# Attention scores of a two-layer graph network: from matmuls on TensorE to a broadcast read from DRAM

## The chip, the cores and the metric

One core of a Trainium2 chip runs the whole kernel as one program. The engines are TensorE (PE, with its weight loads as PEld), VectorE (DVE), ScalarE (ACT), GpSimd (POOL) and SyncE (SP, which issues most transfers). Each engine works through its own queue of instructions in order; semaphores make one wait for another. The metric is device time in microseconds (us) for one execution.

## The reference, cut to what matters

There are 128 independent graphs with 128 nodes and 512 features each, in float32. Layer 0 is an attention over the neighbours of each node with 8 heads of 64 units; layer 1 is two hypergraph convolutions (512 to 1024 to 512) with a layer norm between.

```python
h = relu(layernorm(x))
feats = einsum('bnf,hfu->bhnu', h, W)
e_self = einsum('bhnu,hu->bhn', feats, a_self)
e_neigh = einsum('bhnu,hu->bhn', feats, a_neigh)
dense = leaky_relu(e_self[..., :, None] + e_neigh[..., None, :], 0.2)
dense = dense + NEG_BIG * (1.0 - adj[:, None])
att = softmax(dense, axis=-1)
x = x + relu(einsum('bhij,bhju->bhiu', att, feats) + b)
...
h = relu(layernorm(x))
h = layer_norm(relu(hypergraph_conv(h, adj, W1, b1)), gamma, beta)
x = x + (hypergraph_conv(h, adj, W2, b2) + h_in)
```

Here `h_in` is the h that enters layer 1. The score of head h for the pair of nodes (i, j) is e_self[h, i] + e_neigh[h, j]: an outer sum of two vectors of 128 numbers, made 8 times for each graph.

## The kernel before, in words

**Tiling.** One graph's 128 nodes are the 128 partitions. The attention layer works graph by graph; the hypergraph products work on pairs of graphs (G = 2), with seven block products instead of eight (called u1 to u7 in the first convolution, v1 to v7 in the second). Transposes between a row layout and a column layout go out to DRAM and back in 32x32 blocks: `send` (L484) writes a tile to a DRAM buffer, `fetch` (L493) reads it back with four transfers, `turn` (L506) finishes with DVE's block transpose. This happens to x (the normalized input), p (the softmax), o (the attention output) and r (the hidden layer). For the first DIRECT = 4 graphs and the last LAST ones (p 1, o 1, r 2), `turn` transposes on PE instead.

**Stages of one graph's attention**, by the names that the program gives them: x.load, x.stats, x.rstd, x.relu, x.send, x.fetch, x.turn; f (features, L586: h times W, with 2 x 4 extra columns in each of two halves that give e_self and e_neigh, so 264 columns a half); f.keep (L605: copies the extra columns into a padded tile `pad` and adds the bias into `feats`); e (L626: two transposes of `pad` on PE into eT); e.keep (L635: ACT copies one half into lt, DVE spreads the other into rt); d (L646: four matmuls of 256 columns with only 4 rows each, which add e_self and e_neigh); d.leaky (L666: three ACT passes out of PSUM into sc); d.mask (L674: one POOL add over 1024 columns); d.max (L679: DVE); d.exp and d.exp1 (L684: four Exp passes each); p.send, p.fetch, p.turn; av (L701); av.keep; o.send, o.fetch, o.turn, o.scale, o.add; h.stats, h.rstd, h.relu; z (L743); z.keep; h.add. Each pair adds mask and adjacency stages (mask, adj.*, k) and then the u stages, r.* (hidden layer and its norm), the v stages, and y with its end, `finish` (L946), which also stores the result.

**What sets the order.** The program holds a written-out order. `Order.issue` sorts all stage calls by a number, the place; each engine's queue then holds its instructions in that order. A stage's place for graph n is origin(n) + AT[stage] - sooner. origin(n) is taken from EARLY for the first eight graphs and grows by STEP for each later one; `sooner` is a shift for the first eight graphs (EARLY) and the last six (LATE), by groups of stages. A pair's u, r, v and y stages count from its second graph. The places look like microseconds but nothing waits for a time: they only sort. AFTER (near the end) names which stage has to be called before which.

**Queues.** All transfers, apart from four small rows at the start, are issued by SP, in the order of the places; a send that waits for ACT holds back what stands behind it in SP's queue. TensorE's results lie in PSUM: two banks `ps` that take turns (eT, one part of d, av, z, k, y), a pair of banks `pa` for f and two parts of d, and one bank each for ux, uy, vx, vy (uy or vy also takes a part of d). `feats` has two buffers, `sc` and `pp` one each.

Of the kernel before, what the change touches and what calls it, by code (L numbers as in the profile page):

```python
# [8 lines left out]
F32 = mybir.dt.float32  # L9
# [4 lines left out]
P = 128  # L14
B = 32
# [6 lines left out]
STEP = 19.7  # L22
EARLY = (
    (0, 13.83, 4.99, -3.31, -3.04, -66.56, 23.21, -21.35, -34.93),
    (17.06, 0, 1.56, -0.25, 0, 0, -1.12, -1.26, -1.28),
    (36.59, -0.54, 0, -1.88, -4.09, 11.41, -6.28, -13.24, -68.42),
    (56.49, 0, 16.45, -0.83, 0.38, 0.91, -2.88, -0.08, 3.76),
    (76.1, 0, 0, 0.08, 0.74, -32.13, 32.09, -40.74, -57.65),
    (95.89, -1.62, 5.45, -1.16, 0.13, 0.13, -0.2, 0.28, 0.32),
    (115.32, 0.32, -1.01, 1.31, -0.55, 40.63, 8.4, 17.26, 34.97),  # L30
    (135.24, 2.35, 25.05, 0, 0.25, -0, -0.65, 0, -0.15),
)
LATE = (
    (0, 0, 0, 0, 0, 43.36, 50.78, 44.34),
    (0, 0, 0, -1.28, 0, -2.85, 0, -0.14),
    (0, 0.06, 0.98, 0, 14.76, 8.78, 15.66, 13.25),
    (0, -22.78, 0.48, 0.07, 0.26, -1.59, 0.58, -9.89),
    (0, 0, 1.37, 1.02, 15.36, 13.93, 15.82, 32.72),
    (0, 30.96, 0, -0.45, 0.41, -3.7, -0.45, 0.35),
)  # L40
AT = {
    "x.load": -21.95,
    "x.stats": -15.53,
    "x.rstd": -15.44,
    "x.relu": -11.99,
    "x.send": -10.87,
    "x.fetch": -6.75,
    "x.turn": -5.54,
    "f": 0,
    "f.keep": 3.07,  # L50
    "e": 3.77,
    "e.keep": 3.98,
    "d": 5.46,
    "d.leaky": 6.85,
    "d.mask": 8.25,
    "d.max": 12.88,
    "d.exp": 13.13,
    "d.exp1": 15.17,
    "p.send": 18.81,
    "p.fetch": 20.77,  # L60
    "p.turn": 26.6,
    "av": 29.3,
    "av.keep": 29.4,
    "o.send": 30.82,
    "o.fetch": 36.22,
    "o.turn": 37.55,
    "o.scale": 38.14,
    "o.add": 39.38,
    "h.stats": 42.94,
    "h.rstd": 43.02,  # L70
    "h.relu": 46.17,
    "z": 47.93,
    "z.keep": 51.23,
    "h.add": 51.55,
    "mask.load": -34.65,
    "mask": -21.04,
    "adj.load": -17.12,
    "adj.turn": 13.46,
    "adj.weigh": 17.47,
    "k": 31.81,  # L80
    "k.keep": 38.44,
    "us1": 55.2,
    "us2": 57.58,
    "us3": 55.55,
    "us4": 90.13,
    "u1": 62.85,
    "u1.keep": 70.95,
    "u6": 70.97,
    "u6.keep": 81.26,
    "u2": 76.62,  # L90
    "u2.keep": 78.73,
    "r.aL": 80.04,
    "u5": 83.04,
    "u7": 85.42,
    "u7.keep": 85.87,
    "r.bR": 87.8,
    "u4": 90.51,
    "u4.keep": 95.81,
    "r.bL": 95.88,
    "u3": 90.17,  # L100
    "u3.keep": 92.23,
    "r.aR": 96.21,
    "rb.send": 96.61,
    "rb.stats": 100.31,
    "ra.send": 97.96,
    "ra.stats": 103.65,
    "rb.fetch": 97.63,
    "rb.turn": 102.59,
    "ra.fetch": 101.17,
    "ra.turn": 113.63,  # L110
    "vs1": 112.44,
    "vs3": 117.81,
    "vs2": 120.57,
    "vs4": 137.15,
    "v1": 129.15,
    "v1.keep": 132.3,
    "a1": 133.76,
    "b1": 135.65,
    "b0": 138.73,
    "v6": 140.65,  # L120
    "v6.keep": 141.58,
    "v2": 136.71,
    "v2.keep": 138.23,
    "v5": 144.57,
    "v7": 142.98,
    "v7.keep": 145.72,
    "v4": 152.85,
    "v4.keep": 154.38,
    "v3": 150.71,
    "v3.keep": 151.98,  # L130
    "ya": 161.01,
    "ya.keep": 163.25,
    "yb": 180.67,
    "yb.keep": 182.25,
}
W2_AT = (36.61, -1.28, -6.75, 45.49, 48.27, 57.8, 58.95, 1.45, 76.16, 0.51, 7.04, 6.43, -21.07, -10.31, 0.29, -7.07, -4.88, -5.39)
DIRECT = 4
LAST = {"x": 0, "p": 1, "o": 1, "r": 2}
# [18 lines left out]
def gat_then_hypergraph_kernel(  # L157
# [24 lines left out]
    QH = H // 4  # L182
# [4 lines left out]
    E = 2 * HB  # L187

    const = ctx.enter_context(tc.tile_pool(name="const", bufs=1))
    io = ctx.enter_context(tc.tile_pool(name="io", bufs=11))  # L190
# [56 lines left out]
    for key, v, tile_, at in (  # L247
# [11 lines left out]
    we_sb = wk.tile([P, P], F32, tag="lt", name="we_sb", bufs=1)[:, 0 : KF * 2 * E].rearrange(  # L259
        "p (k b c) -> p k b c", k=KF, b=2  # L260
    )
# [29 lines left out]
    cm = const.tile([P, F], F32, name="cm")  # L291
# [13 lines left out]
    def score_weights(k):  # L305
        for t in range(2):
            prod = wk.tile([P, 2, FB], F32, tag=("xn", "zT")[t], name=f"prod_{t}_{k}", bufs=(1, 3)[t])
            (nc.vector, nc.gpsimd)[t].tensor_tensor(
                prod,
                w0_sb[:, k, :, 0:FB],  # L310
                (a_bc[0], an_bc)[t].rearrange("p (b c) -> p b c", b=2),
                ALU.mult,
            )
            nc.vector.tensor_reduce(
                we_sb[:, k, :, t * HB : (t + 1) * HB],
                prod.rearrange("p b (h u) -> p b h u", u=U),
                AX.X,
                ALU.add,
            )
# [6 lines left out]
    def bias_rows(key, out):  # L326
        spreads.add(key)
        for q in range(out.shape[1] // F):
            t = psum(f"{key}_{q}")
# [3 lines left out]
    def turn_gb():  # L333
        t = psum("gb_ps")
# [4 lines left out]

    EW = P + QH
    pads = []
    for i in range(2):
        pad = const.tile([P, 2 * EW], F32, name=f"pad_{i}")
        nc.vector.memset(pad, 0.0)
        nc.vector.memset(
            pad[:, 0:P].rearrange("p (q y) -> p q y", y=32)[:, :, QH : 2 * QH], 1.0
        )
        nc.vector.memset(  # L350
            pad[:, P : 2 * P].rearrange("p (q y) -> p q y", y=32)[:, :, 0:QH], 1.0
        )
        pads.append(pad)
    dh = const.tile([P, QH], F32, name="dh")
    iq = ident.rearrange("p (q y) -> p q y", y=32)
    for j in range(QH):
        nc.vector.tensor_reduce(
            dh[:, j : j + 1], iq[:, :, j : 2 * QH : QH], AX.XY, ALU.add
        )
    diag = const.tile([P, QH, P], F32, name="diag")  # L360
    nc.vector.tensor_copy(diag, dh.unsqueeze(2).to_broadcast([P, QH, P]))
# [8 lines left out]
    NF = 2  # L370
# [4 lines left out]
    def second_rows():  # L375
        assert "gbT" in sw
        t = psum("sw_ps")[0:2]
# [11 lines left out]
    def second_spread():  # L389
        for i, key in enumerate(("cm", "bw")):  # L390
            sw[key] = psum(f"{key}_ps")
# [7 lines left out]
        nc.scalar.copy(bw_bc, sw["bw"])  # L399
        nc.scalar.mul(cm, sw["cm"], 1.0 / DH)  # L400
# [3 lines left out]
    def second_weights(k):  # L404
        assert "cm" in sw
        sw["centred"] = sw.get("centred", 0) + 1
        nc.vector.scalar_tensor_tensor(
            w2_sb[:, k], w2_sb[:, k], gbT[:, k : k + 1], cm, ALU.mult, ALU.subtract
# [44 lines left out]

    def norm_rstd(n, key):

        mv = sm.tile([P, 2], F32, tag="mv", name=f"mv_{key}{n}")
        nc.vector.bn_aggr(mv, S[n].pop("st" + key))  # L457
# [17 lines left out]
    def direct(n, key):  # L475
        return n < DIRECT or n >= N - LAST[key]

# [6 lines left out]
    def send(n, key, rows, k):  # L484
# [6 lines left out]
        nc.sync.dma_start(d, rows.rearrange("p (b c) -> p b c", b=NB))  # L491
# [14 lines left out]
    def turn(n, key, k, tag, bufs=2):  # L506
        rows = S[n].pop(key + "r")
        S[n][tag] = wk.tile([P, k, P], F32, tag=tag, name=f"{tag}_{n}", bufs=bufs)
        if direct(n, key):
            for q in range(k // 4):  # L510
                t = psum(f"{key}t_{n}_{q}")
# [49 lines left out]
    def adj_keep(g):  # L561
        s = SP[g]
        k_ps = s.pop("k_ps")
        s["kk"] = gp.tile([P, G, P], F32, tag="kk", name=f"kk_{g}", bufs=5)
        nc.scalar.copy(s["kk"], k_ps[:, :, 0:P])

# [38 lines left out]
    def keep_features(n):  # L605
# [3 lines left out]
        pad = pads[n % 2]  # L609
        for t in range(2):  # L610
            nc.vector.tensor_copy(
                pad[:, t * EW : t * EW + P]
                .rearrange("p (b q y) -> p b q y", b=2, y=32)[:, :, :, 0:QH],
# [584 lines left out]
```

## Time and profile before

| what | value |
|---|---|
| median of 3 runs | 2672.8 us (2669.91 to 2674.42) |
| profiled execution, own time | 2671.91 us |
| its span, first to last instruction | 2670.1 us |
| granted TensorE clock, mean | 0.993 |
| busy: PE, PEld, DVE, ACT, POOL | 2611.1, 1799.3, 1907.0, 1500.8, 1855.5 us |
| f (L597), 2048 PE instructions | 486.1 us |
| d (L658), 1024 PE instructions | 92.4 us |
| eT (L631), 256 PE instructions | 49.5 us |
| mask add (L677), 128 POOL instructions | 303.0 us, 2367 ns each |
| DMA moved | 478.5 MB, 179 GB/s mean |

How to read it: the busy time of an engine is the time in which at least one of its instructions ran, so overlapping instructions count once; "mean ns of one" counts each in full. A float32 matmul appears as two instructions: f is written as 8 matmuls and has 16 records a graph. A line of a group names the line of the program, the engine, the operation, the tile written and those read, the shapes, the count, then the busy time, the mean of one, and the idle time of the engine just before such instructions with what ended it. A line of the timeline gives the start, the length and the number of merged instructions. A line of waits gives the total, the number of times and the longest.

### The profile page before, as it was taken

The page shows a single profiled execution, that of the slowest core. Times are in us where ns is not written, and L with a number is a line of the kernel's source. Part 1 is how long each engine was busy: PE and PEld are TensorE (multiplying, and loading weights), DVE is VectorE, ACT ScalarE, POOL GpSimd, SP SyncE. Part 2 cuts the span into 40 slices and gives each one's busy share as a digit, 9 for nine tenths or more (in the row PEclk, how much of TensorE's full clock was granted, in tenths as well). Part 3 has the DMA queues.
Part 4 walks back from the last instruction along what each step waited for, and adds up shares of the span by engine and source line. Part 5 has one row for each costly group of instructions (what it writes and reads, how often), then busy time and mean ns, then how long its engine had stood idle before and what let it go on. Part 6 is the DMA issues. An engine that isn't in the chain of part 4 may idle for free.

```text
span 2670.1 us, 42320 instructions
## 1 busy us (share of the span) xinstructions
PE 2611.1 (98%) x12461; PEld 1799.3 (67%) x12461; DVE 1907.0 (71%) x3554; ACT 1500.8 (56%) x4948; POOL 1855.5 (69%) x2196
## 2 busy tenths in 40 slices
PE   8799999999999999999999999999999999999999
PEld 4466667666667666667666666667666667667666
DVE  4667777777777776777777776777776777777763
ACT  3555556556556555556555555556556556556542
POOL 5676767767767767767767767767767767767763
PEclk8899999999999999999999999999999999999999
DMA  3246656666666666566566566566566566666541
GB/s 111 81 126 194 192 182 199 193 181 194 190 189 196 182 195 195 182 190 199 184 190 198 180 196 194 182 195 195 179 197 196 175 204 196 180 196 194 177 133 59
DMA packets 501616, 478.51 MB, mean 179 GB/s; under 512 B 135797, under 2 KB 404101, under 8 KB 501386
## 3 DMA queue, kind: packets, MB, share of 16 engines
q1 hardware_dynamic: 501376, 475.80, 58.9%
q8 instruction: 99, 1.62, 0.3%
q14 instruction: 131, 1.07, 0.1%
q10 hardware_dynamic: 10, 0.01, 0.0%
HBM read 248.86 MB, written 226.75 MB: 178 GB/s over the span
## 4 chain that ended last, share of the span: by engine, by line
PE 60%; DMA 17%; SPq 8%; DVE 7%; ACT 5%; issue 2%; POOL 1%; DVEq 0%; ACTq 0%; POOLq 0%
PE f L597 12%; PE uy L855 8%; SPq L502 7%; PE vy L855 7%; PE vx L855 6%; DMA pm<-pd 6%; PE uz L855 5%; PE ux L855 5%; PE vz L855 4%; DMA xd<-xn 3%; PE av L707 3%; PE y L946 3%; DMA pd<-pp 2%; DMA rd<-r 2%; PE z L747 2%
## 5 line engine op out<-in xcount | busy, mean ns | idle before, releaser
L597 PE MATMUL f<-w_sb,hT 128*128 128x264 f32 (+1 forms) x2048 | 486.1, 391 | 10.7 <-DVE hT L521 9.6
L597 PEld LDWEIGHTS f<-w_sb,hT 128*128 128x128 f32 x2048 | 391.7, 193 | 113.2 <-issue 34.9
L691 ACT ACTIVATE pp<-sc,nmx 128x128 f32<-128x128 f32 x1024 | 396.8, 391 | 98.6 <-DVE nmx L682 98.6
L677 POOL TENSOR_TENSOR sc<-sc,at 128x1024 f32<-128x1024 f32 x128 | 303.0, 2367 | 62.8 <-ACT sc L672 62.6
L855 PE MATMUL vx<-w_sb,rT 128*128 128x256 f32 x1024 | 248.3, 385 | 0.5 <-DVE rT L519 0.4
L855 PE MATMUL ux<-w_sb,zT 128*128 128x512 f32 x512 | 240.6, 592 | 0.0
L639 ACT COPY lt<-eT 128x128 f32<-128x128 f32 x128 | 34.0, 266 | 355.1 <-PE eT L631 355.1
L733 POOL TENSOR_TENSOR xt<-xt,o 128x512 f32<-128x512 f32 x128 | 163.0, 1274 | 99.0 <-DVE o L729 54.1
L459 POOL TENSOR_SCALAR ve_a<-mv_a 128x1 f32<-128x1 f32 x128 | 28.4, 222 | 272.2 <-DVE mv_a L457 258.0
L855 PEld LDWEIGHTS vx<-w_sb,rT 128*128 128x128 f32 x1024 | 184.7, 190 | 33.3 <-issue 11.8
L521 DVE STREAM_TRANSPOSE pT<-pm 128x1024 f32<-128x1024 f32 x123 | 152.9, 1243 | 66.8 <-DMA pm<-pd 62.4
L691 ACT ACTIVATION_READ_ACCUMULATOR pp<-sc,nmx 128x1 f32 x1024 | 193.9, 189 | 0.0
L790 ACT ACTIVATE sq<-r,nm 128x512 f32<-128x512 f32 x256 | 182.7, 714 | 4.2
L773 ACT ACTIVATE r<-aL 128x512 f32<-128x512 f32 x64 | 40.4, 631 | 253.7 <-DVE aL L866 253.7
L831 POOL TENSOR_TENSOR rT<-rT,rT 128x512 f32<-128x512 f32 x64 | 81.5, 1274 | 137.7 <-DVE rT L521 119.6
L682 DVE TENSOR_REDUCE nmx<-sc 128x8 f32<-128x1024 f32 x128 | 155.3, 1213 | 28.0 <-POOL sc L677 27.7
L765 POOL TENSOR_TENSOR xt<-xt,b_bc 128x512 f32<-128x512 f32 x128 | 163.1, 1274 | 10.0
L521 DVE STREAM_TRANSPOSE hT<-xm 128x512 f32<-128x512 f32 x124 | 88.0, 710 | 114.7 <-DMA xm<-xd 114.6
L469 ACT ACTIVATE h<-xt,nmr_b,rstd_b 128x512 f32<-128x512 f32 x128 | 103.2, 806 | 114.9 <-POOL nmr_b L464 114.9
L764 POOL TENSOR_TENSOR xt<-xt,h 128x512 f32<-128x512 f32 x128 | 163.2, 1275 | 5.2 <-ACT h L469 5.2
L747 PEld LDWEIGHTS z<-kk,h 128*128 128x128 f32 x1024 | 134.6, 193 | 40.4 <-issue 24.8
L641 DVE TENSOR_TENSOR rt<-diag,eT 128x256 f32<-128x256 f32 x128 | 51.9, 405 | 153.6 <-ACT lt L639 153.6
(165 smaller groups left out, 6441.6 us busy)
## 6 DMA issues: line engine op xcount, KB each, us to landing
pd<-pp SPq DMA_DIRECT2D x123, 512.0 KB, 3.8
pm<-pd SPq DMA_DIRECT2D x492, 128.0 KB, 3.7
rd<-r SPq DMA_DIRECT2D x122, 512.0 KB, 3.7
rm<-rd SPq DMA_DIRECT2D x488, 128.0 KB, 3.1
xt<-in_x SPq DMA_DIRECT2D x128, 256.0 KB, 2.9
out<-xt SPq DMA_DIRECT2D x128, 256.0 KB, 2.8
xd<-xn SPq DMA_DIRECT2D x124, 256.0 KB, 2.2
xm<-xd SPq DMA_DIRECT2D x496, 64.0 KB, 2.0
```

The source lines that it names most:

```text
L502: nc.sync.dma_start(m[b * B : (b + 1) * B], d[:, b, :].rearrange("(a x) r -> x a r", x=B))
L521: nc.vector.transpose(S[n][tag].rearrange("p k (a x) -> p k a x", x=B), S[n].pop(key + "m").rearrange("p a (k y) -> p k a y", y=B),)
L597: nc.tensor.matmul(s["f"][:, b, cols], hT[:, k, :], weights[:, k, b, :], start=(k == 0), stop=(k == KF - 1),)
L677: nc.gpsimd.tensor_tensor(s["sc"], s["sc"], neg.to_broadcast([P, H, P]), ALU.add)
L682: nc.vector.tensor_reduce(s["nmx"], s["sc"], AX.X, ALU.max, negate=True)
L691: nc.scalar.activation(blocks(n, "p", s["pp"])[:, h], sc[:, h, :].rearrange("p (b y) -> p b y", y=B), AF.Exp, bias=nmx[:, h : h + 1], accu ...
L733: nc.gpsimd.tensor_tensor(s["xt"], s["xt"], s.pop("o").rearrange("p k c -> p (k c)"), ALU.add)
L747: nc.tensor.matmul(s["z"][:, k * P : (k + 1) * P], s["h1"][:, k * P : (k + 1) * P], SP[n // G]["kk"][:, n % G, :], start=True, stop=True,)
L764: nc.gpsimd.tensor_tensor(s["xt"], s["xt"], s["h1"], ALU.add)
L765: nc.gpsimd.tensor_tensor(s["xt"], s["xt"], b2_bc, ALU.add)
L790: nc.scalar.activation(sq, s["r"][:, q * 512 : (q + 1) * 512], AF.Square, bias=nm[:, 1:2], accum_out=ss[:, q : q + 1],)
L855: nc.tensor.matmul(p[w + bank][:, 0:cols], left[:, k, :], right[:, k, :], start=(first and k == 0), stop=(k == kb - 1), skip_group_check=n ...
```

## The change

The scores are no longer made on PE.

1. The extra columns of f are sorted differently: the first half of f carries e_self of all 8 heads, the second half e_neigh of all 8 (E stays 8). f.keep copies e_self into a small tile `es`. Stage e is now one DVE block transpose of e_neigh's 32 last columns, straight out of PSUM. e.send (SP) writes the 16 KB to DRAM; e.fetch (SP, two transfers) reads 4 heads x 128 numbers, 2 KB, into every one of the 128 partitions, 256 KB each, as the tiles sc (halves, three buffers). The two transposes on PE, `pad`, lt, rt, diag and the four d matmuls are gone.
2. leaky is 8 ACT passes of 128x128 with e_self as the bias, in place in sc. Mask, maximum and Exp work by halves of four heads, so that the second half can follow the first.
3. `send` (x, p, o, r) is issued by ACT. e.send, all fetches, loads and the stores of the result stay with SP; the store of the result is a stage of its own.
4. DIRECT is now 4 for x, p and o and 2 for r, and no last graph is transposed on PE (LAST is gone).
5. Some one-time weight work uses other PSUM banks; `feats` has three buffers in place of two, `io` (the x tiles) 12 in place of 11; norm means, degrees and the hidden norm's root are stages of their own.
6. All places are new: STEP is 19.25 instead of 19.7, EARLY, LATE, AT and W2_AT have new numbers.

```diff
-STEP = 19.7
+STEP = 19.25
...
 AT = {
-    "x.load": -21.95,
+    "x.load": -19.25,
...
-    "x.send": -10.87,
-    "x.fetch": -6.75,
-    "x.turn": -5.54,
+    "x.send": -12.05,
+    "x.fetch": -9.3,
+    "x.turn": -3.58,
     "f": 0,
-    "f.keep": 3.07,
-    "e": 3.77,
-    "e.keep": 3.98,
-    "d": 5.46,
-    "d.leaky": 6.85,
-    "d.mask": 8.25,
-    "d.max": 12.88,
-    "d.exp": 13.13,
-    "d.exp1": 15.17,
-    "p.send": 18.81,
-    "p.fetch": 20.77,
-    "p.turn": 26.6,
-    "av": 29.3,
+    "e": 2.18,
+    "f.keep": 5.65,
+    "e.send": 4.8,
+    "e.fetch": 8.85,
+    "d.leaky": 11.65,
+    "d.leaky1": 12.71,
+    "d.mask": 12.49,
+    "d.mask1": 14.25,
+    "d.max": 14.4,
+    "d.max1": 15.7,
+    "d.exp": 15.25,
+    "d.exp1": 17.1,
+    "p.send": 19.43,
+    "p.fetch": 24.45,
+    "p.turn": 29.56,
+    "av": 33.41,
...
-    "o.send": 30.82,
-    "o.fetch": 36.22,
+    "o.send": 39.2,
+    "o.fetch": 51.02,
...
-    "z": 47.93,
+    "z": 71.55,
...
-    "u1": 62.85,
+    "u1": 81.64,
...
-    "v1": 129.15,
+    "v1": 142.38,
...
-    "yb": 180.67,
-    "yb.keep": 182.25,
+    "yb": 183.16,
+    "yb.keep": 186.01,
+    "yb.store": 186.48,
 }
...
-DIRECT = 4
-LAST = {"x": 0, "p": 1, "o": 1, "r": 2}
+DIRECT = {"x": 4, "p": 4, "o": 4, "r": 2}
...
     def direct(n, key):
-        return n < DIRECT or n >= N - LAST[key]
+        return n < DIRECT[key]
...
     def send(n, key, rows, k):
...
-        nc.sync.dma_start(d, rows.rearrange("p (b c) -> p b c", b=NB))
+        nc.scalar.dma_start(d, rows.rearrange("p (b c) -> p b c", b=NB))
...
     def turn_e(n):
         s = S[n]
-        s["eT"] = psum(f"eT_{n}")
...
+        s["eT"] = sm.tile([P, B], F32, tag="eT", name=f"eT_{n}", bufs=2)
+        nc.vector.transpose(s["eT"], s["f"][:, 1, FB + E - B : FB + E])
+
+    def send_e(n):
+        s = S[n]
+        s["ed"] = dr.tile([B, NB, B], F32, tag="ed", name=f"ed_{n}")
+        nc.sync.dma_start(s["ed"].rearrange("y b x -> b y x"), s.pop("eT"))
+
+    def fetch_e(n):
+        s = S[n]
+        ed = s.pop("ed")
+        s["sc"] = []
+        for part in range(2):
+            sc = wk.tile([P, HB, P], F32, tag="sc", name=f"sc_{n}_{part}", bufs=3)
+            nc.sync.dma_start(
+                sc.rearrange("p h j -> p (h j)"),
+                ed[B - H + part * HB :][0:HB]
+                .rearrange("(o y) b x -> o (y b x)", o=1)
+                .to_broadcast([P, HB * P]),
+            )
+            s["sc"].append(sc)
+
+
+    def leaky(n, part):
+        s = S[n]
+        for j in range(HB):
+            h = part * HB + j
+            sc = s["sc"][part][:, j]
+            nc.scalar.activation(sc, sc, AF.Prelu, bias=s["es"][:, h : h + 1], alpha=SLOPE)
+
+    def mask(n, part):
+        sc = S[n]["sc"][part]
         neg = SP[n // G]["neg"][:, n % G : n % G + 1, :]
-        nc.gpsimd.tensor_tensor(s["sc"], s["sc"], neg.to_broadcast([P, H, P]), ALU.add)
...
+        nc.gpsimd.tensor_tensor(sc, sc, neg.to_broadcast([P, HB, P]), ALU.add)
...
-        nc.sync.dma_start(out[n], s.pop("xt"))
+
+    def store(n):
+        nc.sync.dma_start(out[n], S[n].pop("xt"))
```

## The prediction

> **What bounds the kernel now.** I read the busy times first, then the slices, then TensorE's (PE's) own groups, then its instructions in order of time, and last the queues.
>
> The page's busy times, the slices of PE and its clock, and the shares of the chain that ended last:
>
> ```profile
> PE 2611.1 (98%) x12461; PEld 1799.3 (67%) x12461; DVE 1907.0 (71%) x3554; ACT 1500.8 (56%) x4948; POOL 1855.5 (69%) x2196
> ...
> PE   8799999999999999999999999999999999999999
> ...
> PEclk8899999999999999999999999999999999999999
> ...
> PE 60%; DMA 17%; SPq 8%; DVE 7%; ACT 5%; issue 2%; POOL 1%; DVEq 0%; ACTq 0%; POOLq 0%
> ```
>
> PE is busy for 98% of the span and idle for 59 us in all; only the first slices (the fill) are below nine tenths. A stretch of the steady part says the same (columns: length, then busy time and count of PE, PEld, DVE, ACT, POOL, then clock, DMA share, GB/s):
>
> ```profile
> 1200.00:1600.00 400.00, 397.40 (x1915) 275.28 (x1913) 293.45 (x550) 231.26 (x769) 285.18 (x337) 1.00 0.63 191
> ```
>
> PE lacks 2.6 of 400 us; the next engine, VectorE (DVE), has 107 us free. So the steady part ends when PE's queue ends, and what is taken off PE comes off the time until the next engine or a wait takes over. The ninth product f starts at 161.78 us and the 128th at 2557.39: 2395.6 / 119 = 20.13 us for one graph.
>
> **What the change takes off PE.** The two groups that go, and where they stand in time (start, length):
>
> ```profile
> L658 PE MATMUL d<-rt,lt 4*128 4x256 f32 x1024 | 92.4, 430 | 5.2 <-DVE rt L641 5.2
> L631 PE MATMUL eT<-ident,pad 128*128 128x128 f32 x256 | 49.5, 275 | 8.0 <-DVE pad L611 8.0
> ```
>
> ```profile
> 1317.27 0.38 PE L631 MATMUL eT<-ident,pad 128*128 128x128 f32 x2
> 1317.48 1.88 PE L855 MATMUL uz<-w_t,us 128*128 128x512 f32 x4
> 1319.30 0.71 PE L658 MATMUL d<-rt,lt 4*128 4x256 f32 x8
> 1319.94 1.98 PE L855 MATMUL uy<-w_sb,zT 128*128 128x512 f32 x4
> 1321.76 1.05 PE L747 MATMUL z<-kk,h 128*128 128x128 f32 x8
> ...
> 1325.61 1.88 PE L855 MATMUL uz<-w_sb,us 128*128 128x512 f32 x4
> 1327.32 1.88 PE L855 MATMUL uy<-w_t,zT 128*128 128x512 f32 x4
> 1329.04 0.61 PE L557 MATMUL k<-hmb,hmT 128*128 128x129 f32 x4
> ```
>
> Busy time alone gives (92.4 + 49.5) / 128 = 1.11 us for a graph, but matmuls overlap, so I take distances between starts. eT holds the queue from 1317.27 to 1317.48, 0.21 us; d from 1319.30 to 1319.94, 0.64. An ordinary block of four takes 1.72 (1325.61 to 1327.32 to 1329.04), but the one ahead of d takes 1.82 (1317.48 to 1319.30) and the one behind it 1.82: d costs 0.10 more on each side. Together 0.21 + 0.64 + 0.20 = 1.05 us, between 0.85 (no side costs) and 1.11 (busy). **128 x 1.05 = -134 us** (bounds -109 and -142). Nothing is put on PE in their place; f keeps its 264 columns, since E is 8 before and after. The transposes on PE that DIRECT and LAST ask for become fewer: those of the last p (two blocks of four), o (one) and two r (four), and of r for graphs 2 and 3 (four). Eleven blocks at 0.44 us (8 took 2642.44 to 2643.31) are **-5 us**.
>
> **What it puts elsewhere, for each graph.**
> - ScalarE (ACT): it loses lt (0.27) and the three leaky passes (1.0 from start to end in the queue), and gains eight passes of 128x128 with a bias. The nearest rows are L549 (0.68 for two) and L691 (0.39 each with its accumulator): 2.7 to 3.1. It gains four DMA issues. SP needs 0.34 for such a one, ACT's own in the trace took 0.22 to 0.52: 0.9 to 2.1. ACT goes from 231.3 / 400 x 20.13 = 11.6 us to 14.0 to 15.6.
> - GpSimd (POOL): one mask add of 2.37 becomes two of 512 columns, 1.27 each by the row L764: 14.4 + 0.2 = 14.6.
> - DVE: two pad copies (0.24) and rt (0.41) go; a copy of es (0.16), a transpose of 128x32 (between 0.13 and the 0.43 of the 128x256 one, L536) and one more start of a maximum (0.1) come: 14.8 stays 14.8.
> - DMA: SP's and ACT's transfers use 0.63 x 20.13 = 12.7 us of all 16 engines. The queue's own line
>
> ```profile
> q1 hardware_dynamic: 501376, 475.80, 58.9%
> ```
>
> gives 475.8 MB / (0.589 x 16 x 2670 us) = 18.9 KB per us of one engine, and 50 ns a packet. Two fetches of 256 KB are 524 / (16 x 18.9) = 1.7 us, 128 small packets of e.send 0.4: 14.8.
>
> At 19.1 us for a graph these are 73 to 82% (ACT), 76, 77 and 77%: all under PE's 100, so I price them at nothing beyond the new waits below. The cover is PE's queue; without it, the surplus over 19.1 us would count 128 times.
>
> **The new path to the scores.** Before, f reaches leaky by pad, eT, lt, rt, d. Now: DVE's e at f's end, e.send on SP (0.34 and a landing; the row am, also of 128-byte pieces, lands in 2.6), two e.fetch (0.4 each, landing as xt, 2.9): about 7.5 us from f to the first leaky, against 3.1 before (f ends at 1316.57, leaky starts at 1320.37 behind another pass). Behind e.fetch on SP stands x.fetch, and behind leaky on ACT stand exp, p.send and av.keep: if the row is late, the next f and av are late. The places leave room: e.fetch stands 4.05 behind e.send with p.fetch's four issues between, leaky 2.8 behind e.fetch, and av 33.4 behind f where it was 29.3; feats gets a third buffer for it. Between 0 and the full 4.4 us a graph (a path with no room), I take 0 for the path itself.
>
> By the Trainium skill, "DMA: Bandwidth & Descriptors", section "Why a DMA increments its semaphore by 16 and not by 1", a transfer is split over no more engines than divide both sides' outermost sizes, and e.send writes with the outermost size 4. At 50 ns a packet that would be 1.6 us in place of the 0.4 of 16 engines, my estimate from the row above and that rule; no row here shows it, and it would be 1.2 us of the room.
>
> **Sends in ACT's queue.** SP now waits in its own order for what ACT has yet to finish:
>
> ```profile
> SPq L491 <- ACT oT L718: 212.4, 122, 3.5
> SPq L491 <- ACT xn L469: 165.5, 114, 34.2
> SPq L491 <- ACT r L773: 86.9, 59, 9.4
> ```
>
> On ACT the data were written by the same engine, so these 465 us of SP's waiting go, while ACT pays the issues counted above. SP is 8% of the chain and PE covers it, so I value this at 0. The same page, section "Rules for kernel authors", speaks against the move: issuing from several engines saves only issue time, since all run on the same DMA engines. By it the gain is 0 as well, but the three rows show that waiting in order is what SP sheds.
>
> **Fill and drain.** The first u1 stood at place 79.9 and started at 93.72; its place is now 101.3, 21.3 later. The first v1 goes from 147.5 (started 159.60) to 162.0, 14.5 later. u and v take 7 blocks of 1.72 a pair each, 6.0 a graph, so PE work of 21.3/20 x 6.0 + 14.5/20 x 6.0 = 10.8, with z 12 us, moves from the fill, where PE has gaps, to behind the last f: **+12** (bounds 0, if the fill closes up, and 24). At the end the last r went over PE (0.87 and a copy); now send (3.7), four issues (1.8), landing (3.1) and a transpose (1.2) take 8 us more. The previous pair's v products (12 us) stand in between: **+8** (0 to 16).
>
> **New waits in the steady part.** All places are new and the others' loads rise from 58 to 74% to 73 to 82%. PE idled 14.5 us between 400 and 2400, 0.15 a graph. I add 0.2 for each of 120 graphs: **+24** (bounds 0 and the 1.05 saved, 126).
>
> **Sum**, on the profiled execution's 2671.9 us (0.9 under the median of the runs, 2672.8): 2671.9 - 134 - 5 + 12 + 8 + 24 = **2577 us**, about 3.6% faster.
>
> **Rivals.**
> 1. Another order takes PE's place: DVE, POOL and ACT each stand in one queue, and one late landing holds all behind it. For it: in the first 200 us PE waits for DVE (pad 7.0, rt 5.2 us), so such waits exist. Against: in the steady part only 0.7% is lost at 74%. If half the saving is given back, 0.5 us x 126 more, the time is 2577 + 63 = 2640.
> 2. Slower: the broadcast fetch. 128 partitions read one 2 KB row, which no row here shows. If it costs k times the queue's mean, DMA needs 12.7 + 0.4 + 1.7k; it passes today's 20.13 at k = 4.1 and then sets the pace. At k = 4.5 it is 20.8, and the time 2672 + 0.7 x 120 + 20 (fill and drain) = 2776. For it: DMA is the second largest user and it already reaches eight tenths in some slices of 10 us. Against: p's 512 KB land in 3.8 us.
> 3. No change: the path from f to the scores sets the graph's pace at just 20.1 us, 2673. Little speaks for a hit within 0.2%, which is about what a measurement of this kernel can tell from no change.
>
> **Chances.** Forecast 0.56 (its own range 2540 to 2615), rival 1 0.23, rival 2 0.18, rival 3 0.03. Faster 0.79, same 0.03, slower 0.18. The range for 8 in 10 runs from 2535, where fill, drain and waits cost little, to 2680, past rivals 1 and 3; rival 2 is left out.
>
> **What would show it.** Right: no d and eT on PE; f to f near 19.3 us; PE busy by about 140 us less and still over 95%; u1 starting near 115 us; sc landing about 3 us after its issue; DMA share near 0.75 in the steady part. Wrong: idle PE ahead of f or av put down to hT or pT, DVE or ACT above 90% in the steady part, or sc landing 6 us and more after its issue.

## The result, and the profile after

The changed kernel takes 2657.8 us (median of 5 runs, 2649.8 to 2660.5) where the kernel before took 2674.4 (2669.9 to 2678.0): a ratio of 0.9937, with a 95% interval from 0.9917 to 0.9957. It is faster by 0.6%, where 3.6% was forecast. The profiled execution's own time is 2657.79 us, its span 2656.0, the granted clock 0.986 (0.993 before).

The lines of the page after that answer to those of before: busy times, slices of PE and its clock, the two queues (SP's is q1, ACT's is q10) and the landing of the broadcast (count, KB each, median us from issue to landing).

```profile
PE 2492.6 (94%) x11137; PEld 1752.2 (66%) x11137; DVE 1841.8 (69%) x3545; ACT 1664.3 (63%) x5455; POOL 1865.5 (70%) x2324
...
PE   6689999999999999999999999999999999999998
...
q1 hardware_dynamic: 487744, 354.68, 48.9%
q10 hardware_dynamic: 71722, 196.13, 19.1%
...
sc<-ed SPq DMA_DIRECT2D x256, 256.0 KB, 3.8
```

The same stretch of the steady part (length; busy time and count of PE, PEld, DVE, ACT, POOL; clock; DMA share; GB/s):

```profile
1200.00:1600.00 400.00, 383.14 (x1725) 270.69 (x1724) 286.85 (x553) 260.63 (x856) 289.22 (x362) 1.00 0.71 219
```

PE did 118.5 us less work, which is the change's aim, and the slices still show it at nine tenths. But in this stretch it now lacks 16.9 of 400 us, where it lacked 2.6. A slice of 66 us rounds that away; the stretch and the waits show it. The next busiest engine, POOL, stands at 72% and ACT at 65%: none has become the bound.

**Where the time went**, from the starts of f in both traces:

| part | before | after | difference |
|---|---|---|---|
| start of the ninth f | 161.78 | 176.81 | +15 |
| ninth to 128th f, 119 graphs | 2395.6 (20.13 each) | 2358.6 (19.82 each) | -37 |
| last f to the end of the span | 112.7 | 120.6 | +8 |

The sum is the -14 by which the spans differ. PE's busy time in the stretch of the 119 graphs, first before, then after:

```profile
161.78:2557.39 2395.61, 2376.06 (x11456) 1647.91 (x11455) 1763.35 (x3279) 1388.73 (x4602) 1700.76 (x2024) 1.00 0.63 189
```

```profile
176.81:2535.44 2358.63, 2265.09 (x10240) 1603.81 (x10241) 1699.20 (x3273) 1539.38 (x5063) 1707.63 (x2141) 1.00 0.72 220
```

PE was idle there for 19.6 us before and 93.5 after, 0.16 and 0.79 us a graph. What PE itself needs for a graph went from 19.97 to 19.03, which is 0.93 less, and 0.62 of that came back as waiting: 119 x (0.62 - 0.93) = -37. PE's waits between 400 and 2400 us (total us, times, longest), before and after:

```profile
PE av L707 <- DVE pT L521: 7.1, 16, 1.3
PE f L597 <- DVE hT L521: 6.4, 13, 1.2
PE eT L631 <- DVE pad L611: 0.5, 1, 0.5
```

```profile
PE uy L830 <- DVE bR L841: 43.0, 50, 2.6
PE av L678 <- DVE xt L928: 27.3, 23, 1.7
PE uy L830 <- POOL us L806: 10.2, 14, 1.5
PE f L589 <- DVE hT L509: 0.6, 1, 0.6
```

The few waits of before, for pT ahead of av and for hT ahead of f, have almost gone, and the scores do not appear at all: no line says that PE waits for sc. What PE waits for now are u7.keep (bR: DVE frees the bank that the next block of u wants), the end of y (xt: DVE frees the bank that av wants), and POOL's operands for u. All three are small operations that stand behind something else in their engine's queue. One case in order of time, first PE, then DVE:

```profile
1329.37 3.80 PE L589 MATMUL f<-w_sb,hT 128*128 128x264 f32 x16
1333.01 0.61 PE L545 MATMUL k<-hmb,hmT 128*128 128x129 f32 x4
1335.50 1.98 PE L830 MATMUL uy<-w_t,zT 128*128 128x512 f32 x4 [1.88 <-DVE bR L841]
1337.32 1.02 PE L830 MATMUL uz<-w_sb,us 128*128 128x512 f32 x2
```

```profile
1332.67 1.25 DVE L509 STREAM_TRANSPOSE rT<-rm 128x1024 f32<-128x1024 f32 x1 [0.65 <-DMA rm<-rd]
1333.84 0.65 DVE L436 BATCH_NORM_STATS2 st_b<-xt 128x6 f32<-128x512 f32 x1
1334.53 0.18 DVE L441 BATCH_NORM_AGGREGATE mv_b<-st_b 128x2 f32<-128x6 f32 x1
1334.62 0.18 DVE L616 STREAM_TRANSPOSE eT<-f 128x32 f32<-128x32 f32 x1
1334.73 0.71 DVE L841 SCALAR_TENSOR_TENSOR bR<-uy,dn,bR 128x512 f32<-128x512 f32 x1
```

DVE waits 0.65 us for rm, a landing that has nothing to do with u. Behind it in the order stand r's transpose, the statistics, e's new transpose and only then bR. PE waits 1.88 us. So what PE waits for by the view is DVE; of that, 0.65 us is DVE's own wait for a transfer, and the rest is what stands ahead of bR in DVE's order.

### The profile page after: what moved, and what is told of

It is laid out like the page before. It is cut to its first block, busy times and chain, and to the rows that moved or that the text cites. A ratio compares the mean times of both kernels' runs of the same rounds, so it can differ in the third digit from the quotient of the medians.

```text
span 2656.0 us, 41199 instructions
## 1 busy us (share of the span) xinstructions
PE 2492.6 (94%) x11137; PEld 1752.2 (66%) x11137; DVE 1841.8 (69%) x3545; ACT 1664.3 (63%) x5455; POOL 1865.5 (70%) x2324
## 5 line engine op out<-in xcount | busy, mean ns | idle before, releaser
L643 ACT ACTIVATE sc<-sc,es 128x128 f32<-128x128 f32 x1024 | 318.9, 391 | 146.8 <-DMA sc<-ed 135.1
L648 POOL TENSOR_TENSOR sc<-sc,at 128x512 f32<-128x512 f32 x256 | 322.8, 1272 | 121.9 <-ACT sc L643 120.2
L457 ACT ACTIVATE xn<-xt,nmr_a,rstd_a 128x512 f32<-128x512 f32 x128 | 104.2, 814 | 305.9 <-POOL nmr_a L452 290.6
L653 DVE TENSOR_REDUCE nmx<-sc 128x4 f32<-128x512 f32 x256 | 173.0, 676 | 144.3 <-POOL sc L648 141.0
L830 PEld LDWEIGHTS vx<-w_sb,rT 128*128 128x128 f32 x1024 | 194.4, 190 | 83.6 <-issue 46.3
L678 PE MATMUL av<-pT,feats 128*64 128x128 f32 x2048 | 142.3, 281 | 42.2 <-DVE xt L928 31.5
L830 PE MATMUL uy<-w_t,zT 128*128 128x512 f32 x256 | 128.9, 627 | 53.9 <-DVE bR L841 53.9
L689 ACT ACTIVATE oT<-av 128x512 f32<-128x512 f32 x128 | 75.1, 586 | 155.3 <-PE av L678 154.6
L509 DVE STREAM_TRANSPOSE rT<-rm 128x1024 f32<-128x1024 f32 x126 | 155.7, 1236 | 23.2 <-DMA rm<-rd 22.4
L928 DVE SCALAR_TENSOR_TENSOR xt<-y,dn,xt 128x512 f32<-128x512 f32 x128 | 95.6, 747 | 96.3 <-PE y L921 96.0
```

Of the source, the lines that this page charges most:

```text
L509: nc.vector.transpose(S[n][tag].rearrange("p k (a x) -> p k a x", x=B), S[n].pop(key + "m").rearrange("p a (k y) -> p k a y", y=B),)
L643: nc.scalar.activation(sc, sc, AF.Prelu, bias=s["es"][:, h : h + 1], alpha=SLOPE)
L648: nc.gpsimd.tensor_tensor(sc, sc, neg.to_broadcast([P, HB, P]), ALU.add)
L653: nc.vector.tensor_reduce(s["nmx", part], s["sc"][part], AX.X, ALU.max, negate=True)
L678: nc.tensor.matmul(s["av"][side * U : (side + 1) * U, j * P : (j + 1) * P], feats[n % NF][:, h * U : (h + 1) * U], pT[:, h, :], start=True ...
L830: nc.tensor.matmul(p[w + bank][:, 0:cols], left[:, k, :], right[:, k, :], start=(first and k == 0), stop=(k == kb - 1), skip_group_check=n ...
```

## The experiments

Five theories of the lost 0.62 us a graph were tried, in this order. **1:** each wait of PE is one stage in a bad place of DVE's order; moved, its wait goes. **2:** the broadcast's bytes make all landings late, and a late landing holds an engine that works in order (the prediction's first rival). **3:** adj.load, whose issues stand ahead of e.fetch in SP's order, makes the scores late. **4:** x.load is issued too late. **5:** the whole chain of x stands too late. The runs were made on several chips, on which the kernel before took 2656.9 to 2674.4 us, so each time is given as a ratio to the kernel before on the same chip, with its interval. "Idle" is the sum of PE's waits between 400 and 2400 us.

The changed kernel itself was run again on two of these chips, beside other runs:

> The changed kernel once more, unaltered, as the base for the other kernels on the same chip. Both theories: its ratio to the kernel before stays at 0.9937, within 0.9917 to 0.9957.

> The changed kernel unaltered, the base for the three others on this chip. Its ratio to the kernel before was 0.9937 and 0.9881; all theories: between 0.985 and 0.996.

It gave 0.9881 [0.9861, 0.9902] with 55 us idle, and 0.9903 [0.9889, 0.9918] with 64. With the first 0.9937 and 81, three chips give 0.988 to 0.994: differences between chips are larger than one run's interval, so a variant means something only beyond that band.

**u7_first**: u7.keep ahead of h.stats and e on DVE.

```diff
-    "u7.keep": 99.35,
+    "u7.keep": 96.75,
```

> The changed kernel with one place altered: u7.keep goes from 99.35 to 96.75, so that on DVE it stands ahead of h.stats and of e, which waits for f's end; u4 on PE waits for u7.keep. Theory 1 (order on DVE): between 400 and 2400 us PE idles 43 us ahead of u4; that goes, 0.43 us x 120 graphs = 51 us, about 2607, and the wait of uy on bR is under 10 us. Theory 2 (the broadcast fetch makes landings late and DVE late as a whole): the wait shows up again ahead of other products, and the time stays above 2640.

1.0035 [1.0024, 1.0046], idle 79. The wait for bR went from 43 to 2.3 us, as theory 1 says, and another of the same size took its place:

```profile
PE vx L830 <- ACT b L884: 37.1, 38, 1.5
PE av L678 <- DVE xt L928: 30.6, 25, 2.3
```

This run also prices a wait. Here PE mostly goes from k to the block of u without one:

```profile
1370.44 0.61 PE L545 MATMUL k<-hmb,hmT 128*128 128x129 f32 x4
1370.88 1.88 PE L830 MATMUL uy<-w_t,zT 128*128 128x512 f32 x4
1372.60 1.88 PE L830 MATMUL uz<-w_sb,us 128*128 128x512 f32 x4
```

The block of u starts 0.44 us after k and the next block 1.72 later. In the case above with its wait, k's 0.61 us run out in full, and the block holds the queue for 1.82 (1335.50 to 1337.32). So a wait at this place costs about 0.27 us more than the idle time that it shows.

**adj_later**: two adjacency stages that stand ahead of the end of y.

```diff
-    "adj.turn": 29.78,
-    "adj.weigh": 31.52,
+    "adj.turn": 31.6,
+    "adj.weigh": 32.5,
```

> The changed kernel with two places altered: adj.turn from 29.78 to 31.6 and adj.weigh from 31.52 to 32.5, so that DVE's five adjacency passes (about 2 us a pair) stand behind ya.keep, whose result frees the PSUM bank that av takes. Theory 1 (order on DVE): PE's 27 us ahead of av between 400 and 2400 go, 0.27 x 120 = 32 us at most, about 2630. Theory 2 (late landings push DVE): the wait moves elsewhere, under 10 us gained, above 2645.

0.9852 [0.9838, 0.9867], idle 50. The wait of av is gone, that for bR stayed at 41.8. It is the fastest kernel here that computes the whole reference, and faster than the kernel before. That it beats the changed kernel isn't shown: its interval overlaps that of the changed kernel's best chip, 0.9861 to 0.9902.

**half_rows**: each e.fetch reads half the rows, 1 KB into each partition, and each row serves two heads, so four of the eight heads get another head's neighbour scores.

```diff
-                ed[B - H + part * HB :][0:HB]
+                ed[B - H + part * HB :][0 : HB // 2]
...
-                .to_broadcast([P, HB * P]),
+                .to_broadcast([P, HB // 2 * P]),
...
-            nc.scalar.activation(sc, sc, AF.Prelu, bias=s["es"][:, h : h + 1], alpha=SLOPE)
+            nc.scalar.activation(sc[:, j], sc[:, j % 2], AF.Prelu, bias=s["es"][:, h : h + 1], alpha=SLOPE)
```

> The changed kernel with half of the broadcast: each e.fetch brings the rows of two heads, 1 KB a partition instead of 2 KB, and leaky uses them twice; so e_neigh of four of the eight heads is left out of the scores, all ACT, POOL, DVE and PE work stays. Theory 2 (transfers): DMA share falls from 0.73 to about 0.68, the landings come earlier, and at least 40 us go, under 2618. Theory 1 (order on DVE): the stalls of u4 and av stay, less than 12 us go, above 2645.

0.9779 [0.9764, 0.9793], idle 41. The same instructions in the same order, with 33.6 MB less, are 1.0 to 1.6% faster than the changed kernel on its three chips. Not every landing is shorter: x's fetch, which stands behind the broadcast on SP, lands in 2.7 us in place of 3.1 (median), the adjacency's load in 3.8 in place of 5.3, p's fetch in 2.9 in both. The waits of PE are the same two, both shorter:

```profile
PE uy L830 <- DVE bR L841: 26.0, 52, 0.6
PE av L678 <- DVE xt L928: 15.2, 16, 1.0
```

What is left of the wait for bR is no landing's doing. It is 0.5 us in 51 of the 52 cases, with DVE ready and idle until f ends, since bR stands right behind e:

```profile
1338.98 0.22 DVE L616 STREAM_TRANSPOSE eT<-f 128x32 f32<-128x32 f32 x1 [1.99 <-PE f L589]
1339.12 0.71 DVE L841 SCALAR_TENSOR_TENSOR bR<-uy,dn,bR 128x512 f32<-128x512 f32 x1
```

In the changed kernel, too, each of the 50 waits for bR is at least 0.49 us, so some 25 of their 43 us are this place in DVE's order, and the other 18 lateness.

**d_narrow**: one part alone, on the kernel before. The d matmuls make 8 columns in place of 256, and leaky reads those 8 over and over, so the scores of the other columns are left out; the rest is unchanged.

```diff
-                outs[q],
+                outs[q][:, 0:8],
...
-                rt[rows].rearrange("k h j -> k (h j)"),
+                rt[rows].rearrange("k h j -> k (h j)")[:, 0:8],
...
```

> The kernel before with the four score matmuls cut from 256 to 8 columns, and leaky reading those 8 columns over and over (a broadcast read), so most scores are left out while every other instruction stays. It prices PE time in the old order. If PE's queue is the bound there, as the forecast took it, d's 0.84 us a graph falls to 0.3 to 0.5 and the time by 128 x 0.34 to 0.54 = 44 to 69 us, to 2603 to 2629. If the old order's other queues hold the pace, less than 15 us go.

0.9930 [0.9915, 0.9945]: 18 us gained, idle 8. The distance from d to the next block fell from 0.64 to 0.33, 40 us for 128 graphs, so less than half of it arrived although PE stayed full. Some 9 us went to the block behind d, which in one graph of two takes 1.97 us in place of 1.83. Where the rest went isn't settled: the profile of the kernel before is of another chip, on which it took 2671.9 us and not 2658.4.

**adjload_early** (theory 3) and **adj_both** (with adj_later's edit):

```diff
-    "adj.load": 25.02,
+    "adj.load": 21.5,
```

> The changed kernel with adj.load's place altered from 25.02 to 21.5: on SP the adjacency loads of a pair (2.3 us of issues) now stand ahead of e.send, where SP waits 3.7 us a graph for f to end, and no longer between e.send and e.fetch. It also changes which earlier transfer's completion the second e.fetch of that graph waits for (DMAs share eight semaphores in turn): it was x.send, issued by ACT for the next graph. Theory 3 (the path from f to the scores is stretched by what stands between e.send and e.fetch on SP, and its lateness reaches PE through DVE): sc lands at least 2.3 us earlier in one graph of two, SP's wait of L629 on xd goes from 67 to under 15 us between 400 and 2400, and 15 to 40 us of time go against the changed kernel. Theory 1 (the order on DVE alone): less than 8 us.

> The changed kernel with both alterations: adj.load at 21.5 (ahead of e.send on SP) and adj.turn at 31.6, adj.weigh at 32.5 (behind ya.keep on DVE). Alone the second brought 23 us (0.9852 against 0.9937 of the kernel before). Theory 1 (order on DVE): the same 23 us as alone, ratio about 0.985. Theory 3 (path to the scores as well): 35 to 60 us, ratio 0.971 to 0.981.

1.0698 [1.0646, 1.075] and 1.0091 [1.0058, 1.0124]: both slower than the changed kernel, the first by far. SP's queue and PE's in adjload_early, 400 to 2400 us:

```profile
SPq L242 <- DMA pd<-pp: 170.8, 47, 5.4
```

```profile
PE av L678 <- DVE xt L928: 143.1, 47, 5.5
```

The adjacency load reads nothing of p, yet waits for p.send to land. In the compiled program, the transfers of SP's and ACT's queues take eight completion semaphores in turn (the trace names eight for both queues), and one that takes a semaphore waits until its last user has landed. So the place of a load decides which transfer of the other queue it waits for; here that was p.send, and e.send, p.fetch and e.fetch stood behind it. The changed kernel has such waits too (L629 is e.fetch, which reads nothing of x):

```profile
SPq L629 <- DMA xd<-xn: 67.3, 44, 4.0
```

In adjload_early this wait has gone, as theory 3 said, but the scores are no earlier (9.1 us from f's end to the first leaky, 8.8 to 9.0 in the changed kernel), so the theory is not tested by it.

**sends_on_sp**: part 3 of the change undone, in the new order.

```diff
-        nc.scalar.dma_start(d, rows.rearrange("p (b c) -> p b c", b=NB))
+        nc.sync.dma_start(d, rows.rearrange("p (b c) -> p b c", b=NB))
```

> The changed kernel with one part undone: the sends of x, p, o and r are issued by SP again, at the same places. My forecast valued the move at 0: then the time stays within 8 us of the changed kernel. Theory 3 (what stands ahead of e.fetch on SP decides): x.send then stands ahead of e.fetch in every graph and SP waits for ACT's xn there; 20 us or more slower.

1.0471 [1.0454, 1.0488], 155 us more than the changed kernel on the same chip, idle 144. SP's waits, 400 to 2400 us:

```profile
SPq L479 <- ACT xn L457: 149.0, 49, 3.4
SPq L490 <- DMA rd<-r: 141.2, 48, 4.7
SPq L490 <- DMA xd<-xn: 114.4, 96, 3.2
SPq L621 <- DVE eT L616: 82.4, 50, 3.5
SPq L479 <- ACT pp L662: 82.0, 56, 2.3
```

With the sends back, SP waits for ACT (L479) as it did before the change, and now for f's end (L621) as well. These places were made for sends on ACT, so 155 us is the price in this order, not in every order.

**two_stalls** (u7.keep at 97.9 and adj_later's edit) and **two_half** (the same with half_rows's edit):

> The changed kernel with both PE stalls taken at their place on DVE: u7.keep from 99.35 to 97.9 (behind h.mean, ahead of e, so that it runs while f still does and h.stats is not held up), and adj.turn, adj.weigh at 31.6 and 32.5 (behind ya.keep). Base: the changed kernel at 0.988 of the kernel before on a chip of this speed. Theory 1 (local order on DVE): PE's 33 us ahead of u4 and 19 ahead of av between 400 and 2400 both go, 45 to 60 us over the run, ratio 0.966 to 0.972. Rival (the sum of late landings sets the pace; a stall that is taken away comes back at the next place): at most 15 us, ratio over 0.982, with new waits ahead of v products as in the run with u7.keep first.

> The kernel with the two DVE stalls taken, and half of the broadcast (1 KB a partition instead of 2 KB, so e_neigh of four of the eight heads is left out of the scores). If transfers set what is left (theory 2): another 20 us or more below the kernel with two_stalls. If local order was the whole loss (theory 1): within 8 us of it.

On one chip, 1.020 [1.0179, 1.0222] with 113 us idle, and 0.9855 [0.9834, 0.9877] with 51. Both stages that PE waited for now stand earlier, and the kernel is slower than with neither moved; PE waits in two_stalls:

```profile
PE uy L830 <- POOL us L806: 69.1, 46, 2.8
PE uy L830 <- DVE bR L841: 40.0, 39, 2.0
```

Theory 1 as a whole falls here: a wait has a part that is its stage's place, as the 0.5 us of bR, but with the stage moved, others grow. And in this order half the broadcast's bytes are worth 94 us.

**xload_early** (x.load from -19.25 to -23.5) and **all_three** (with two_stalls's edits):

> The changed kernel with x.load's place altered from -19.25 to -23.5, 4.25 earlier on SP. x.stats stands 3.7 behind x.load, while the load now takes 4.7 us to land, and ACT waits 220 us between 400 and 2400 for the norm of the next graph with r.bL, v1.keep and the next leaky behind it. If that late load sets the pace (theory 4): ACT's wait of xn on nmr falls under 120 us and 15 us or more go, ratio under 0.982. If the two DVE stalls alone do (theory 1): within 6 us of the changed kernel, ratio 0.985 to 0.991.

> The alterations of the two kernels ahead of this one together: u7.keep at 97.9, adj.turn and adj.weigh at 31.6 and 32.5, x.load at -23.5. Theory 1: as with the two DVE stalls alone, 0.966 to 0.972. Rival (stalls move on): the early load keeps ACT from becoming the next place, so at least 10 us better than the two stalls alone.

0.9946 [0.9926, 0.9967] and 1.0221 [1.0196, 1.0247], each no better than without the earlier load (0.988 to 0.994, and 1.020). Theory 4 falls.

**x_ahead** moves all of x's stages up to the send forward by 2.05 to 5.75, **x_ahead_adj** adds adj_later's edit and **x_ahead_two** two_stalls's.

```diff
-    "x.load": -19.25,
-    "x.stats": -15.55,
+    "x.load": -25,
+    "x.stats": -17.6,
...
-    "x.relu": -13.05,
-    "x.send": -12.05,
+    "x.relu": -15.3,
+    "x.send": -15.28,
```

> The changed kernel with the x stages earlier: x.load -25, x.stats -17.6, x.mean -17.5, x.rstd -17.2, x.relu -15.3, x.send -15.28 (from -19.25, -15.55, -14.6, -14.03, -13.05, -12.05). On DVE x.stats of the next graph now stands ahead of e, not behind it, and on ACT xn ahead of h.relu. Theory 5 (the loop from f to f through e and x.stats sets the pace): SP's wait of x.fetch on xd falls from 220 us to under 100 between 400 and 2400, PE's idle time there under 40 us, and the time by 20 to 50 us against the changed kernel on this chip. Theory 1 (local stalls of PE alone): u4 and av wait as before, within 8 us.

> The x stages earlier as in x_ahead, and adj.turn and adj.weigh at 31.6 and 32.5, behind ya.keep, as in adj_later. Theory 5: PE's wait ahead of av goes too; 5 to 25 us below x_ahead. Theory 2 (transfers set the pace): within 5 us of the changed kernel.

> The x stages earlier, adj.turn and adj.weigh later, and u7.keep at 97.9, ahead of e. Without the x stages earlier this was 2 to 3% slower than the changed kernel. Theory 5: u7.keep ahead of e put 1.5 us into the loop, which now has room, so the loss goes: within 10 us of x_ahead_adj or below it. If e.send's lateness (SP) and not x.stats carries the loss: still 30 us or more above x_ahead_adj.

1.0292 [1.0269, 1.0314], 1.0302 [1.0273, 1.0332] and 1.0387 [1.037, 1.0404]. Theory 5 falls: ACT now stood 306 us of 2000 at x.relu (234 in the changed kernel) waiting for POOL's part of the norm, with other work behind it.

**half_plus_load** and **load_only**: what half_rows gained could come from the scores landing earlier or from fewer bytes. Two loads of 128 KB a graph that nobody reads were added to half_rows and to the changed kernel, away from the scores' path.

```diff
+    def spare(n, i):
+        xx = wk.tile([P, F // 2], F32, tag="xx", name=f"xx_{n}_{i}", bufs=1)
+        nc.sync.dma_start(xx, x[n][0:1, 0 : F // 2].to_broadcast([P, F // 2]))
...
         nc.sync.dma_start(S[n]["xt"], x[n])
+        spare(n, 0)
...
     def fetch(n, key, k):
+        if key == "x":
+            spare(n, 1)
```

> The changed kernel with half the rows read in each e.fetch (1 KB to each partition; each row serves two heads, so four of the eight heads get another head's neighbour scores), as in half_rows, and two more loads of 128 KB a graph (a 1 KB row of x read by all partitions, into a tile that nobody reads), one behind x.load and one ahead of the x fetch. The bytes of a graph are those of the changed kernel, and the scores' own path is that of half_rows. Load theory (the added traffic on the DMA engines makes the other landings late): 0.988 to 0.994 of the kernel before, as the changed kernel had, and TensorE idle between 400 and 2400 us 55 to 80 us. Path theory (what counts is how early the scores land, for the engines that wait for them in order): 0.975 to 0.983, as half_rows had, and idle near 41 us.

> The changed kernel, all its rows fetched as they were, with the same two added loads of 128 KB a graph as half_plus_load. Load theory: slower than the changed kernel by about as much as half_rows was faster, 1.000 to 1.015 of the kernel before, idle above 85 us. Path theory: 0.986 to 0.996, no different from the changed kernel, idle 55 to 80 us. If both this and half_plus_load come out slower than 1.0, the added instructions in SyncE's order or the completion semaphores they take, and not bytes, are what costs.

0.9946 [0.9931, 0.9961] with 73 us idle, and 1.031 [1.0281, 1.0339] with 122. With the bytes put back elsewhere, all that half_rows had gained is lost. But this doesn't part the two theories, since the added loads made the scores' path longer as well: from f's end to the first leaky it was 8.1 us in half_rows, 8.7 in half_plus_load, 8.8 to 9.0 in the changed kernel and 9.9 in load_only (means of graphs 21 to 118). Against the path alone stands two_half, in another order: 9.45 us, longer than in the changed kernel, and 51 us of idle time. What grows with the loads is DVE's waiting for landings, here in load_only, 400 to 2400 us:

```profile
DVE hT L516 <- DMA xm<-xd: 139.5, 73, 4.4
...
DVE st_a L441 <- DMA xt<-in_x: 59.6, 39, 3.0
...
DVE pT L516 <- DMA pm<-pd: 51.0, 57, 2.5
```

Summed over all landings and set beside PE's idle time, for the kernels that share the changed kernel's order of places:

| kernel | DVE's waits for landings, us of 2000 | PE idle, us of 2000 |
|---|---|---|
| half_rows | 139 | 41 |
| changed kernel, three chips | 162, 176, 205 | 55, 64, 81 |
| half_plus_load | 219 | 73 |
| load_only | 315 | 122 |

load_only lost more than the 1.000 to 1.015 that the load theory expected. Part of it is not bytes: e.send waited 233.7 us for p.send's landing, which it doesn't read, so the semaphores' turn has a share. Which share is open, in half_plus_load too, since an added load is at once bytes, an issue on SP and one more turn. And the table holds for one order only: in the kernel before, DVE waits 173 us for landings and PE is idle 14; in two_half it is 309 and 51. DVE waits for landings about as long as before the change (162 to 205 us), so the waiting alone doesn't make PE idle; what stands behind it counts as well.

## Why the prediction was right in sign and wrong in size

The forecast took 95 us off the profiled execution's 2671.9; the spans differ by 14. The time lies inside the wide range, above the forecast's own. The 81 us between them split into three.

- **New waits in the steady part: the step that failed.** It took 0.2 us a graph, +24. Measured are 0.62 a graph, +74 over 119 graphs: 50 us. The reason it gave, that every engine but PE would stay under 85%, was true (ACT 65% without its issues, POOL 72, DVE 72, DMA 71) and no protection. What it did not look at is the order on DVE: bR, which frees a bank for PE, was put behind e, which waits for f's end, and this alone is 0.5 us of idle time in each pair, some 30 of the 74 us. The first rival had named the mechanism of another part, one late landing that holds all behind it in an in-order queue. Its size was near, too: 24 + 63 = 87 us of waits against 74; that it fits so well is in part luck, since the place of bR was not in it, and that the time came out above its 2640 is due to the next two terms.
- **Fill and drain**, 17 us together. Ahead of the ninth f the terms were 9 x 1.05 and four transposing blocks (1.8) less: -11, and it came to +15. PE did have 12 us less work there (130.8 busy before, 119.0 after), but it was idle for 27 more, so what it is spared among the gaps of the fill isn't saved; the first u1 started at 119.84, 26 later, where 21.3 was forecast. Behind the last f they were +12 for moved work and +8, less seven blocks (3): +17, and it came to +8.
- **What PE is spared** was 0.93 a graph in place of 1.05: 14 us. By the starts of the blocks in both traces, the 1.05 itself did go: eT, d and the 0.10 on each side of d, since a pair has four fewer blocks that take 1.81 to 1.83 in place of 1.72. What came back is the part of the waits for bR that idle time doesn't show, 0.27 us a pair as in u7_first, 0.13 a graph. So this shortfall, too, belongs to the new waits.

Other steps. **The broadcast** landed in 3.8 us against about 3 (the page's figure is the one landing of 256 that the profile could tell; where ACT stood waiting for sc, 60 times in graphs 21 to 118, it was 3.8 from issue to leaky, at most 5.6), and DMA stood at 0.71 to 0.72 against 0.75; the second rival, the fetch as the pace, did not occur. But the bytes, priced by the DMA engines' share alone, cost more than that: half of them are worth 1.0 to 1.6% in this order and 3.5% in another. **The path to the scores** was put at 7.5 us; the shortest took 7.5 and the mean 8.8 to 9.0, since e.send and e.fetch stand behind others in SP's order. Its room held as far as PE goes: no wait of PE names it, though ACT waited 103 us of 2000 for sc. The landing of e.send, for which the prediction gave an estimate, is not on the page; e.fetch waited for it 6.8 us in all. But the path's first link was not looked at: e.send stands in SP's queue and waits for f's end, and p.fetch, e.fetch and x.fetch stand behind it.

```profile
SPq L621 <- DVE eT L616: 505.7, 125, 15.2
```

That is as much as the 465 us of waits for ACT that the sends took away with them. **The sends in ACT's queue** were valued at 0, with the words that PE's queue covers SP. sends_on_sp gives 155 us in the new order. The page "DMA: Bandwidth & Descriptors" of the Trainium skill, section "Rules for kernel authors", which the prediction weighed, lets the move save issue time alone; here, with the sends back, SP waited 149 and 82 us of 2000 for ACT, the in-order waiting that the prediction's three rows had shown. That this is all of the 155 us isn't shown, since the turn of the semaphores changes as well.

What remains of the cause: that the broadcast's bytes cost time in the steady part is shown by half_rows and two_half, and that bR's place behind e costs 0.5 us of idle time a pair, whatever lands, by half_rows and u7_first. That moving one stage is no cure is shown by u7_first and two_stalls. That the bytes cost by late landings, which in-order queues pass on to PE, is argued from DVE's waits; the scores' own path got shorter with the bytes, so its share is open. How the rest of the 0.62 divides between the bytes, the semaphores' turn and the places is not settled.

## What to carry to other kernels

When work is taken off an engine that was full, it is no longer enough that every other engine has room on average: list for each new wait what stands behind it in its queue (a send that waits for a matmul's end holds every fetch behind it), and price it. A transfer that PE never seems to wait for can still cost it time; halving its bytes in a trial that leaves data out is a cheap way to find its price. Count a wait above the idle time that it shows: it can also cost the overlap of two matmul blocks, here 0.27 us. Moving the one stage that the profile names first can move the wait to the next, as in u7_first and two_stalls.

## What the runs showed of the hardware

**The clock falls after short idle times of PE.** A block of u (x4 in the timeline) takes 1.98 us behind a wait. In the changed kernel it always did after idle times of up to 1.9 us; after 2.56 us it took 3.47 once and 2.55 once. In the stretch of the first the granted clock (last column but two) was 0.55:

```profile
1494.60:1498.00 3.40, 3.38 (x5) 1.58 (x6) 2.58 (x8) 1.43 (x3) 3.14 (x5) 0.55 0.56 151
```

In two_stalls, six of the 13 idle times between 1.9 and 2.15 us were followed by a slow block. So a long wait is paid again: 1.5 us more for this one. By the Trainium skill, "TensorE: Matmul & The Clock Gate", section "HAM oscillation — how this bites in real kernels", the rule is to leave no idle gap above about 3.4 us; here gaps well below that were followed by a slow block, so in this kernel 2 us is already too long.

**Transfers of two queues wait for each other** through the completion semaphores that they take in turn: 170.8 us of SP's time in adjload_early, 233.7 in load_only, none of it for data.

**ACT's issue of a transfer** holds ACT for about 0.4 us, which its busy time leaves out. The pass ahead of x.send ends at 1319.45, the issue takes 0.33 from 1319.48, and the next pass starts at 1319.85. The prediction had counted 0.22 to 0.52.
